# A decoder block on one core: when the third feed-forward layer's weights are loaded, and where the last pair's norm steps stand

## The chip, the core and the metric

The kernel runs on one core of a Trainium2 chip. A core has five engines, each with its own instruction queue that is worked off in order: PE (TensorE, matrix products), DVE (VectorE), ACT (ScalarE), POOL (GpSimd) and SP (SyncE, here only for sending DMAs). They wait for each other through semaphores. Operands lie in the on-chip memory SBUF, PE writes to PSUM, and 16 DMA engines move data from and to HBM. A DMA can be sent from SP, ACT or POOL; one sent from POOL occupies POOL while it is issued.

The metric is the device time in microseconds (us) of one execution, as the median of several runs. The profile comes from one more execution; its times count from the first instruction (the span's start).

## What is computed

A decoder block on `x` of 32 sequences, 128 tokens and 256 features: causal linear self-attention, cross-attention to a context, and a gated feed-forward network, each behind a layer norm and added to `x`. Cut to the part that matters here:

```python
def ffn(x, w1_w, w1_s, w2_w, w2_s, h1_w, h1_s, h2_w, h2_s, w3_w, w3_s):
    tlin = lambda x, w, s: jnp.einsum('bsi,oi->bso', x, w) * s
    h = silu(tlin(x, w1_w, w1_s)) * tlin(x, w2_w, w2_s)      # 256 -> 1024, the gate
    h = gelu(tlin(h, h1_w, h1_s))                            # 1024 -> 1024
    h = gelu(tlin(h, h2_w, h2_s))                            # 1024 -> 1024
    return tlin(h, w3_w, w3_s)                               # 1024 -> 256

x = x + linear_attention(layernorm(x), ...)
x = x + cross_attention(layernorm(x), context, ...)
x = x + ffn(layernorm(x), ...)
```

The feed-forward weights are small whole numbers, the rest is float32.

## The kernel before

**Stages.** The 32 sequences are 16 pairs for the two attentions and 8 blocks of four sequences (512 tokens) for the feed-forward network. A loop over 20 steps (`for m in range(STEPS)`) runs the attentions as a pipeline over the pairs: in step m the self-attention works on pair m, the cross-attention on pair m - 3, and the norm's statistics on the pairs behind and ahead. Then a loop over the 8 blocks (`for blk in range(NBLK)`) runs the feed-forward network.

**Order.** What each step emits, and in which order, is written out by hand in lists of units (`both`, `close`, `begins`, `alone`, `last`, `rest`), one list a step; `give` walks a list. Most functions are generators: every mention of a unit in a list runs it up to its next `yield`, so that PE's part, ACT's part and POOL's part of one unit can stand apart. PE, ACT, DVE and POOL execute in just the order in which the code emits (`manual_schedule`).

**Filling.** While the last attention steps leave PE free, parts of block 0 of the feed-forward network are run early: `fills` holds its input (transposes), the 8 column groups of the gate (`ffn_gate`) and the first three column groups c = 0, 1, 2 of H1 (`ffn_gelu`). `beside` starts the next fill (its matmuls), `settle` finishes those begun (activation and split).

**Split.** Products run in fp32r, with the activations as a sum of two parts, each multiplied by the same weights. `split` makes them: `gh` (or `sh`, `xh`) is the value cast by POOL, `gl` (`sl`, `xl`) the remainder, taken by the engine passed as `low_engine`: in the fills that is POOL, afterwards DVE. `hidden` multiplies: for each of the 8 slices k of a weight, one matmul with the high and one with the low part. So a column group of H1 or H2 takes 16 matmuls, and each of them needs gh and gl of one column group of the layer before. The unsplit `hg` and `hs` share three buffers.

**Norm.** `norms(k)` holds, for the pairs that end a stage in step k, the statistics (`bn_stats` on DVE), the start of the inverse square root on DVE (`deviations` up to its `yield`, lines 147 to 152), and three Newton steps of four small operations each on POOL (lines 156 to 162), which write `devs`. In the last step, k = 19, only pair 15 is left, whose statistics serve the feed-forward norm of block 7. There the unit is mentioned six times: the first two only pass empty parts, the third runs the statistics and the start, the fourth the Newton steps, the other two nothing.

**Weights of the feed-forward network.** W1, W2 and H1 are loaded during the attentions. H2 (8 slices of 512 KB) and W3 (8 slices of 128 KB) lie in memory that the cross-attention held until then: after the step loop, `left.close()` releases it, and new pools are opened there (lines 845 to 849). The tile framework gives each load the waits for what was there before (`reuse_waits="tile"`): in the built program the first H2 load waits for eight semaphores of earlier SP and ACT loads, one of an earlier POOL load, and one of PE, for the last `pf` matmul of the cross-attention. `load_some` (line 859) sends up to three of the 16 slices, from POOL, and `layer` calls it ahead of each column group (line 870): in block 0, H1 continues with c = 3, so the first three slices are sent ahead of the column group c = 3, the next three ahead of c = 4, and so on. POOL's DMAs take eight semaphores in turn, and a DMA waits until the one before it on its semaphore has landed; so the load of W3 slice k waits for H2 slice k.

POOL's order before, from the last cross-attention add (line 662): gh and gl of c = 2, twelve Newton operations, H2 x3, gh of c = 3, H2 x3, gh of c = 4, H2 x2 and W3 x1, gh of c = 5, W3 x3, gh of c = 6, W3 x3, gh of c = 7, W3 x1.

Of the kernel before, what the change touches and what calls it, by code (L numbers as in the profile page):

```python
# [22 lines left out]
HC = HID // P  # L23
# [5 lines left out]
STEPS = NPAIR + SKEW + 1  # L29
# [18 lines left out]
def decoder_block_kernel(  # L48
# [14 lines left out]
    nc = tc.nc  # L63
# [24 lines left out]
    C_PAR, C_PARS, C_BQ, C_BK, C_W1, C_W2, C_H1, C_H2 = 0, 2, 4, 6, 8, 16, 24, 32  # L88
# [5 lines left out]
    def batch(b):  # L94
        return xs[b // 2][:, b % 2, :]

    W1, W2, H1 = (
        const.tile([P, w.shape[0] // P, w.shape[1]], F32R, name=n) for n, w in (("W1", w1T), ("W2", w2T), ("H1", h1T))
    )
# [10 lines left out]
    def load(n, dst):  # L110

        which, k, width = FFN_SLICES[n]
        nc.gpsimd.dma_start(out=dst[:, k, :], in_=(w1T, w2T, h1T, h2T, w3T)[which][ts(k, P), :])
# [62 lines left out]
    G_TAGS = X_TAGS + ["r20", "r21"] + [f"l{i}" for i in range(10)]  # L176
# [5 lines left out]
    def temporary(tag, name, bufs):  # L182
        return hid["r"].tile([P, TB], F32, tag=tag, name=name, bufs=bufs)
# [6 lines left out]
    def split(t, name, tags, high_engine=nc.gpsimd, low_engine=nc.vector):  # L190

        high, low = part(f"{name}h", tags[0]), part(f"{name}l", tags[1])
        (high_engine.copy if high_engine is nc.scalar else high_engine.tensor_copy)(high, t)  # L193
        lows.append(lambda: low_engine.tensor_tensor(low, t, high.bitcast(F32), ALU.subtract))  # L194
        return high, low

    def finish():
        while lows:
            lows.pop(0)()
# [13 lines left out]
    def ffn_input(xns, res):  # L213
        pts = []
        for c in range(DC):
            pt = ffn_bank("pt")
            for j in range(NB):
                nc.tensor.transpose(pt[:, ts(j, S)], xns[j // 2][:, j % 2, ts(c, P)], ident)  # L218
            pts.append(pt)
        yield  # L220
        for c in range(DC):
            res.append(split(pts[c], "x", X_TAGS[2 * c : 2 * c + 2], nc.scalar))
        finish()

    def hidden(w, src, c):
        pp = ffn_bank("ph")
        for k, parts in enumerate(src):
            for p in range(2):
                nc.tensor.matmul(  # L229
                    pp,  # L230
                    lhsT=w[:, k, ts(c, P)],
                    rhs=parts[p],
                    start=(k == 0 and p == 0),
                    stop=(k == len(src) - 1 and p == 1),
                )
        return pp

    def ffn_gate(src, c, res, low_engine=nc.vector):

        one, two = hidden(W1, src, c), hidden(W2, src, c)  # L240
        yield
        sil = temporary("sil", "sil", 2)
        nc.scalar.activation(sil, one, AF.Silu, scale=col[:, C_W1 + c : C_W1 + c + 1])  # L243
        t = temporary("h", "hs", 3)
        nc.vector.scalar_tensor_tensor(t, two, col[:, C_W2 + c : C_W2 + c + 1], sil, ALU.mult, ALU.mult)  # L245
        finish()
        res.append(split(t, "s", S_TAGS[2 * c : 2 * c + 2], low_engine=low_engine))

    def ffn_gelu(w, src, c, c_scale, tags, res, low_engine=nc.vector):
        pp = hidden(w, src, c)  # L250
        yield
        t = temporary("h", "hg", 3)
        nc.scalar.activation(t, pp, AF.Gelu, scale=col[:, c_scale + c : c_scale + c + 1])  # L253
        res.append(split(t, "g", tags[2 * c : 2 * c + 2], low_engine=low_engine))
        finish()

    def whole(parts):
        for _ in parts:
            pass
# [13 lines left out]
    with tc.manual_schedule(engines=ORDERED):  # L273
# [413 lines left out]
        def settle():  # L687
# [105 lines left out]
        rest = [  # L793
            (b_weighted, -1, 1), (b_weighted, -1, 1), (norms, 0), (b_weighted, -1, 1), (norms, 0),
            (b_weighted, -1, 1), settle, beside, (b_out, -1, 1), (b_out, -1, 1), (b_out, -1, 1), settle,
            (norms, 0), (norms, 0), (norms, 0), (norms, 0),
        ]

        def give(units, m):
# [18 lines left out]
        under_way = {}  # L818
        FILLS = 1 + HC + 3
        block, begun = {"x": [], "s": [], "g": []}, []  # L820
        fills = [lambda: ffn_input(block["xn"], block["x"])]
        fills += [lambda c=c: ffn_gate(block["x"], c, block["s"], nc.gpsimd) for c in range(HC)]
        fills += [lambda c=c: ffn_gelu(H1, block["s"], c, C_H1, G_TAGS, block["g"], nc.gpsimd) for c in range(FILLS - 1 - HC)]

        Bs[0]["c"] = cT0
        done = {(b_load, 0)}
# [25 lines left out]
        def weights(n):  # L852
            return (W1, W2, H1, H2, W3)[FFN_SLICES[n][0]]
# [5 lines left out]
        def load_some():  # L859
            for _, n in zip(range(3), loading):  # L860
                load(n, weights(n))

        def raw():
            return temporary("sil", "raw", 2)

        def layer(blk, w, src, c_scale, tags, res):

            waiting = None
            for c in range(len(res), HC):
                load_some()  # L870
                parts = ffn_gelu(w, src, c, c_scale, tags, res)
                if (blk or w is H2) and c % 4 == 0:
                    n = next(testing, None)
                    waiting = None if n is None else (weights(n), *again(raw, n))
                whole(parts)
                if waiting and c % 4 == 3:
                    test(*waiting)
# [18 lines left out]
        for blk in range(NBLK):  # L896
# [13 lines left out]
            block = {"x": [], "s": [], "g": []}  # L910
# [147 lines left out]
```

## Time and profile before

| | us |
|---|---|
| median of 3 runs | 1097.52 |
| lowest and highest | 1096.7 and 1099.23 |
| the profiled execution | 1099.32 |
| its span, first to last instruction | 1097.3 |
| PE, busy in the span | 1081.9 |
| DVE, busy | 609.9 |
| POOL, busy | 416.4 |
| ACT, busy | 377.8 |
| first H2 load issued, at | 472.3 |
| third layer of block 0 begins on PE, at | 481.8 |
| mean TensorE clock granted, of full speed | 0.996 |

How to read it: the step loop takes the first 464 us or so, the feed-forward blocks the rest. The page's second part shows PE at 9 tenths or more in nearly every slice, from the first to the last:

```profile
PE   8999999999999999999999999999999999999997
DVE  5888888888888877523433433433433432423421
POOL 4565555555555446652312312312312312312311
DMA  7001000011110000050010010010011000000000
```

Each digit is the busy share, in tenths, of one fortieth of the span (27 us). The DMA row's 5 is the slice from about 466 to 494 us: the loads of H2 and W3. The kind of each load and its time from issue to landing (KB each, median us):

```profile
H<-in_h1T_dram POOLq DMA_DIRECT2D x8, 512.0 KB, 3.6
H<-in_h2T_dram POOLq DMA_DIRECT2D x8, 512.0 KB, 7.2
W<-in_w3T_dram POOLq DMA_DIRECT2D x8, 128.0 KB, 5.6
```

H1's slices, sent one at a time, take 3.6 us; H2's, sent together, 7.2 in the median.

### The profile page before, as it was taken

To read this page: it belongs to the slowest core of one execution; us is meant where nothing else is said; L and a number is where in the kernel's file an instruction comes from. 1 tells how busy PE (TensorE), PEld (TensorE's weight loads), DVE (VectorE), ACT (ScalarE), POOL (GpSimd) and SP (SyncE) were. 2 spreads that over 40 slices of the span, in tenths; PEclk is the share of its full clock that TensorE was granted. 3 is DMA by queue.
4 is the path that set the end of the run, shared out by engine and by line. 5 is a ranking of instruction groups with operands and counts; after the bars stand their busy time and mean duration, and the time that the engine had idled before them with its cause. 6 is when DMAs were issued, how large, how long until landed. Compare 5 with 4: busy or idle time off the path is not lost.

```text
span 1097.3 us, 19468 instructions
## 1 busy us (share of the span) xinstructions
PE 1081.9 (99%) x7990; PEld 878.0 (80%) x7990; DVE 609.9 (56%) x1249; ACT 377.8 (34%) x594; POOL 416.4 (38%) x778
## 2 busy tenths in 40 slices
PE   8999999999999999999999999999999999999997
PEld 6777777777777777778888888888888888888886
DVE  5888888888888877523433433433433432423421
ACT  3234444444444459722322312322322312222221
POOL 4565555555555446652312312312312312312311
PEclk9999999999999999999999999999999999999999
DMA  7001000011110000050010010010011000000000
GB/s 265 1 30 31 30 31 30 31 30 42 38 31 30 12 11 1 21 192 24 34 39 29 30 39 30 29 39 35 24 39 39 20 30 20 10 10 20 11 1 22
DMA packets 26544, 39.23 MB, mean 36 GB/s; under 512 B 2512, under 2 KB 18640, under 8 KB 26448
## 3 DMA queue, kind: packets, MB, share of 16 engines
q1 hardware_dynamic: 22000, 26.09, 7.1%
q0 software_dynamic: 4032, 11.54, 3.3%
q8 instruction: 65, 1.06, 0.4%
q14 instruction: 31, 0.25, 0.1%
q10 hardware_dynamic: 416, 0.28, 0.1%
HBM read 33.71 MB, written 4.19 MB: 35 GB/s over the span
## 4 chain that ended last, share of the span: by engine, by line
PE 92%; POOL 3%; DVE 2%; DMA 1%; issue 1%; ACT 0%; POOLq 0%; DVEq 0%; ACTq 0%
PE ph L229 51%; PE pp L373 10%; PE py L882 6%; PE pf L418 5%; PE pv L381 5%; PE sa L402 4%; PE sm L402 3%; PE se L402 3%; PE pw L381 2%; PE pt L362 1%; DVE at L541 1%; PE pot L657 1%; DMA H<-in_h2T_dram 1%; PE se L633 1%; PE pz L618 1%; PE pt L218 1%
## 5 line engine op out<-in xcount | busy, mean ns | idle before, releaser
L194 DVE TENSOR_TENSOR gl<-hg,gh 128x512 fp32r<-128x512 f32 x125 | 86.9, 695 | 336.5 <-POOL gh L193 333.6
L193 POOL CAST gh<-hg 128x512 fp32r<-128x512 f32 x128 | 79.5, 621 | 359.6 <-ACT hg L253 359.6
L253 ACT ACTIVATE hg<-ph,col 128x512 f32<-128x512 f32 x128 | 88.3, 690 | 365.0 <-PE ph L229 364.9
L229 PE MATMUL ph<-gh,H 128*128 128x512 f32 x512 | 200.3, 391 | 1.1 <-POOL gh L193 0.6
L229 PE MATMUL ph<-gl,H 128*128 128x512 f32 x512 | 200.3, 391 | 0.2 <-DVE gl L194 0.2
L229 PE MATMUL ph<-sh,H 128*128 128x512 f32 x512 | 199.6, 390 | 0.0
L229 PE MATMUL ph<-sl,H 128*128 128x512 f32 x512 | 199.2, 389 | 0.0
L229 PEld LDWEIGHTS ph<-gh,H 128*128 128x128 f32 x512 | 96.6, 189 | 22.0 <-POOL gh L193 1.1
L229 PEld LDWEIGHTS ph<-gl,H 128*128 128x128 f32 x512 | 96.7, 189 | 20.7 <-DVE gl L194 0.5
L229 PEld LDWEIGHTS ph<-sh,H 128*128 128x128 f32 x512 | 96.1, 188 | 20.4 <-issue 0.5
L229 PEld LDWEIGHTS ph<-sl,H 128*128 128x128 f32 x512 | 96.1, 188 | 19.9
L229 PE MATMUL ph<-xh,W 128*128 128x512 f32 x256 | 100.7, 393 | 0.0
L229 PE MATMUL ph<-xl,W 128*128 128x512 f32 x256 | 99.8, 390 | 0.0
L193 POOL CAST sh<-hs 128x512 fp32r<-128x512 f32 x64 | 58.7, 917 | 67.5 <-DVE hs L245 67.5
L541 DVE TENSOR_TENSOR at<-sa,causal 128x1024 f32<-128x1024 f32 x64 | 74.5, 1206 | 15.2 <-PE sa L402 11.9
L608 DVE TENSOR_REDUCE nm<-sm 128x8 f32<-128x1024 f32 x64 | 75.0, 1213 | 12.2 <-PE sm L402 12.2
L644 ACT ACTIVATE pr<-se 128x1024 f32<-128x1024 f32 x64 | 62.0, 1020 | 30.2 <-PE se L633 30.2
L245 DVE SCALAR_TENSOR_TENSOR hs<-ph,col,sil 128x512 f32<-128x512 f32 x64 | 47.9, 749 | 41.3 <-PE ph L229 20.7
L500 ACT ACTIVATE e<-pp,col 128x256 f32<-128x256 f32 x64 | 26.9, 471 | 127.4 <-PE pp L373 96.8
L243 ACT ACTIVATE sil<-ph,col 128x512 f32<-128x512 f32 x64 | 44.1, 690 | 74.9 <-PE ph L229 74.8
L373 PE MATMUL pp<-xTa,WA 128*128 128x256 f32 x256 | 62.5, 388 | 0.7 <-ACT xTa L365 0.7
L882 PE MATMUL py<-W,gh 128*128 128x256 f32 x256 | 62.6, 285 | 0.0
(131 smaller groups left out, 1839.0 us busy)
## 6 DMA issues: line engine op xcount, KB each, us to landing
x<-in_x_dram SPq DMA_DIRECT2D x16, 256.0 KB, 5.5
cT<-in_ctxT_dram SPq DMA_DIRECT2D x16, 256.0 KB, 2.6
H<-in_h1T_dram POOLq DMA_DIRECT2D x8, 512.0 KB, 3.6
H<-in_h2T_dram POOLq DMA_DIRECT2D x8, 512.0 KB, 7.2
out_dram<-y SPq DMA_DIRECT2D x32, 128.0 KB, 1.7
raw<-in_h1T_dram SPq DMA_DIRECT2D x16, 256.0 KB, 2.6
raw<-in_h2T_dram SPq DMA_DIRECT2D x16, 256.0 KB, 2.6
WA<-in_wattn_dram SPq DMA_DIRECT2D x4, 256.0 KB, 4.8
```

The costliest lines, as they stand in the source:

```text
L193: (high_engine.copy if high_engine is nc.scalar else high_engine.tensor_copy)(high, t)
L194: lows.append(lambda: low_engine.tensor_tensor(low, t, high.bitcast(F32), ALU.subtract))
L229: nc.tensor.matmul(pp, lhsT=w[:, k, ts(c, P)], rhs=parts[p], start=(k == 0 and p == 0), stop=(k == len(src) - 1 and p == 1),)
L253: nc.scalar.activation(t, pp, AF.Gelu, scale=col[:, c_scale + c : c_scale + c + 1])
L373: nc.tensor.matmul(pp[:, c, :], lhsT=w[:, d, ts(c, P)], rhs=src[:, d, :], start=(d == 0), stop=(d == DC - 1))
L381: nc.tensor.matmul(pp, lhsT=src[:, d, :], rhs=w[:, d, :], start=(d == 0), stop=(d == DC - 1))
L402: nc.tensor.matmul(sc[g // 2][:, g % 2, 2 * c : 2 * c + 2, :], lhsT=loaded[32 * g : 32 * g + 32, c, ts(j, S)], rhs=streamed[32 * g : 32 * ...
L418: nc.tensor.matmul(pf[32 * g : 32 * g + 32, i, :], lhsT=v[:, 8 * (i // 2) + 2 * g + i % 2, :], rhs=weights[g // 2][:, g % 2, i, :], start= ...
L541: nc.vector.tensor_tensor(at.rearrange("p g i s -> p (g i) s"), sc[u].rearrange("p g i s -> p (g i) s"), causal.unsqueeze(1).to_broadcast( ...
L608: nc.vector.tensor_reduce(nm[:, 2 * u : 2 * u + 2, :], sc[u], AX.X, ALU.max, negate=True)
L644: nc.scalar.activation(pr, sc[u], AF.Exp)
L882: nc.tensor.matmul(py[:, :D], lhsT=h[k][p][:, ts(j, S)], rhs=W3[:, k, :], start=(k == 0 and p == 0), stop=(k == HC - 1 and p == 1),)
```

## The change

Three edits.

- In the last step's list `rest`, the unit `(norms, 0)` is mentioned three times in place of six: it stops behind the start of the inverse square root.
- Right behind the opening of the new pools, `load_some` is called twice, which sends H2 slices 0 to 5 in a row; then the rest of `norms(19)`, the Newton steps, is emitted. `layer` goes on with what is left: H2 slices 6 and 7 and W3 slice 0 ahead of c = 3, W3 slices 1 to 3 ahead of c = 4, 4 to 6 ahead of c = 5, 7 ahead of c = 6.
- The remainder gl of the third H1 fill (c = 2) is taken by DVE, those of c = 0 and 1 by POOL as before.

POOL's order then: gh of c = 2, H2 x6, twelve Newton operations, H2 x2 and W3 x1, gh of c = 3, W3 x3, gh of c = 4, W3 x3, gh of c = 5, W3 x1, gh of c = 6, gh of c = 7. On DVE, gl of c = 2 stands between the last transpose of the cross-attention (line 450) and the last pair's statistics (line 139). The order on PE, ACT and SP is the same, and so are the waits of the first H2 load.

```diff
         rest = [
             (b_weighted, -1, 1), (b_weighted, -1, 1), (norms, 0), (b_weighted, -1, 1), (norms, 0),
             (b_weighted, -1, 1), settle, beside, (b_out, -1, 1), (b_out, -1, 1), (b_out, -1, 1), settle,
-            (norms, 0), (norms, 0), (norms, 0), (norms, 0),
+            (norms, 0),
         ]
...
-        fills += [lambda c=c: ffn_gelu(H1, block["s"], c, C_H1, G_TAGS, block["g"], nc.gpsimd) for c in range(FILLS - 1 - HC)]
+        fills += [
+            lambda c=c: ffn_gelu(H1, block["s"], c, C_H1, G_TAGS, block["g"], nc.vector if c > 1 else nc.gpsimd)
+            for c in range(FILLS - 1 - HC)
+        ]
...
         def load_some():
             for _, n in zip(range(3), loading):
                 load(n, weights(n))
+
+        for _ in range(2):
+            load_some()
+
+        whole(under_way.pop((norms, STEPS - 1)))
 
         def raw():
             return temporary("sil", "raw", 2)
```

## The prediction

> **What bounds the kernel now.** I read the page's busy row first, then the chain of waits, then the timelines of POOL and PE where that chain leaves PE. Columns of the chain: start, length in us, what; of a timeline: start, length, engine, line, operation, count, and in brackets the idle time before it with its releaser.
>
> ```profile
> PE 1081.9 (99%) x7990; PEld 878.0 (80%) x7990; DVE 609.9 (56%) x1249; ACT 377.8 (34%) x594; POOL 416.4 (38%) x778
> ...
> 467.06 1.29 POOL gl L194
> 474.59 1.53 POOL H L113 x3
> 476.63 8.41 DMA H<-in_h2T_dram
> 487.25 27.52 PE ph L229 x113
> 514.77 3.83 PE py L882 x32
> ```
>
> PE is the bound, and after 487 us the chain is PE alone to the end: what moves there moves the end one for one. The stretch that isn't PE runs from 464.3 to 487.3: POOL's work, the issue of the H2 loads, then their landing. But most of that stretch is slack, since PE has the second layer (H1) to do meanwhile. What is lost must be read from PE:
>
> ```profile
> 484.34 0.39 PE L229 MATMUL ph<-gl,H 128*128 128x512 f32 x1
> 485.18 0.47 PE L229 MATMUL ph<-gh,H 128*128 128x512 f32 x1 [0.45 <-DMA H<-in_h2T_dram]
> 485.48 0.40 PE L229 MATMUL ph<-gl,H 128*128 128x512 f32 x1
> 486.53 0.50 PE L229 MATMUL ph<-gh,H 128*128 128x512 f32 x1 [0.65 <-POOL gh L193]
> 487.25 0.50 PE L229 MATMUL ph<-gl,H 128*128 128x512 f32 x1 [0.22 <-DVE gl L194]
> 487.59 0.48 PE L229 MATMUL ph<-gh,H 128*128 128x512 f32 x1
> 487.86 0.63 PE L229 MATMUL ph<-gl,H 128*128 128x512 f32 x1
> ```
>
> Third layer, first column block: 16 matmuls from 481.83, a (gh, gl) pair for each slice k = 0 to 7 of H2. Starts are 0.227 apart until 484.34. Then PE waits for slice 6 of H2, and for gh and gl of k = 7. The next block should begin at 481.83 + 16 x 0.2267 = 485.46 and begins at 487.59: **2.13 us lost by waiting**. Then starts are 0.43 apart until 490.85, and the clock says why (stretch: busy time and count of PE, PEld, DVE, ACT, POOL; then PEclk, DMA share, GB/s):
>
> ```profile
> 440.08:443.49 3.41, 2.33 (x44) 1.58 (x46) 3.31 (x6) 3.29 (x4) 2.36 (x5) 1.00 0.02 5
> 484.45:487.86 3.41, 2.09 (x7) 0.97 (x6) 1.35 (x4) 0.07 (x1) 1.82 (x4) 0.98 1.17 310
> 487.86:491.27 3.41, 3.41 (x10) 2.67 (x9) 1.32 (x3) 0.61 (x1) 0.62 (x1) 0.52 0.16 39
> ```
>
> The stretch with the pauses is followed by one of equal length at half clock. The tenth matmul after 487.59 starts at 491.46: 3.87 for 10 steps instead of 2.27, so **1.60 us more**. Together 3.73 us.
>
> Why did slice 6 and gh of k = 7 come so late? POOL:
>
> ```profile
> 466.37 0.61 POOL L193 CAST gh<-hg 128x512 fp32r<-128x512 f32 x1 [1.25 <-ACT hg L253]
> 467.06 1.29 POOL L194 TENSOR_TENSOR gl<-hg,gh 128x512 fp32r<-128x512 f32 x1
> ...
> 472.26 1.71 POOL L113 DMA_DIRECT2D H<-in_h2T_dram  x3 [0.62 <-issue]
> 473.95 0.64 POOL L193 CAST gh<-hg 128x512 fp32r<-128x512 f32 x1
> 474.51 1.61 POOL L113 DMA_DIRECT2D H<-in_h2T_dram  x3
> ...
> 484.06 0.53 POOL L113 DMA_DIRECT2D W<-in_w3T_dram  x1 [0.69 <-DMA H<-in_h2T_dram]
> 485.32 0.53 POOL L113 DMA_DIRECT2D W<-in_w3T_dram  x1 [0.73 <-DMA H<-in_h2T_dram]
> 485.85 0.62 POOL L193 CAST gh<-hg 128x512 fp32r<-128x512 f32 x1
> ```
>
> The 12 small Newton operations on `t` and `devs` fill 468.31 to 471.64 (the "..."); only then is the first H2 load issued. The second cost is POOL's order: the issue of W3 slice k waits until H2 slice k has landed (they share a semaphore), and gh of k = 7 stands behind W3 slice 6, thus behind H2 slice 6 (landed 485.04).
>
> **The change part by part.**
>
> *gl of c = 2 goes from POOL to DVE.* POOL is rid of 1.29 us. On DVE the operation takes 0.69 to 1.05 us (its rows at 476.77 and 474.62) and starts when gh is cast, 466.98. It stands ahead of the last pair's statistics, which end by about 467.7 + 1.8 = 469.5 instead of 466.34: DVE had nothing to do until 474.62, so this is hidden. PE reads this gl only at 482.96. Cost nothing; if that cover were gone, 1 us.
>
> *Newton behind six loads.* Its 12 operations (3.33 us) are not removed, they leave the way of loads 0 to 5. Their result is read by the norm of the last block only (the last of those reads starts at 975.7). Nothing to pay there.
>
> *Six loads at once.* The first H2 load now follows the cast that ends at 466.98; with the same 0.62 for its waits (ten semaphores; the newest is that of the last `pf` matmul, done at 459.76) it starts at 467.60 instead of 472.26, **4.66 us earlier**. Six issues take 0.63 + 0.54 + 3 x 0.55 + 0.57 = 3.39: to 470.99. Newton to 474.32. Then loads 6 and 7 and W3 slice 0 (0.56 + 0.57 + 0.58): to 476.03.
>
> *Landings.* Before, slices 0 to 7 landed 3.6, 5.2, 7.8, 9.0, 10.3, 11.5, 12.8 and 14.0 us after the first issue (issue plus time to landing); the last six are 1.2 to 1.3 apart, the queue being full. Loads 6 and 7 are issued at 474.3, some 5 us before slice 5 lands (479.1), so the queue doesn't run dry: slice 6 at 480.4, slice 7 at 481.6. PE wants slice 6 at 484.55 and slice 7 at 485.00. That wait goes.
>
> *What queues behind.* gh of c = 3 now comes at 476.03, two us later than 473.95. PE wants it at 483.2. ACT does earlier: `hg` has three buffers, so ACT's hg of c = 6 (478.40) needs gl of c = 3, done at 476.03 + 0.65 + 0.75 = 477.4: 1 us spare. Next, W3 slices 1 to 3 (by 477.8), gh of c = 4 (by 478.5), W3 slices 4 to 6; slice 6 must wait for H2 slice 6: 480.4 + 0.28 + 0.53 = 481.2. Then gh of c = 5 (481.85), W3 slice 7 behind H2 slice 7: 481.6 + 0.28 + 0.53 = 482.4, then gh of c = 6 (483.05), gh of c = 7 (483.75) and its gl on DVE (484.45). PE wants gh of c = 6 at 484.55, gl at 484.78; gh of c = 7 at 485.00, gl at 485.23. All in time, by 0.7 us at the tightest. Written with L for the landing of H2 slice 7: the last gl reaches PE at L + 2.9, so no wait as long as L is below 482.3.
>
> *Sum.* Loads 4.66 earlier, but only the wait can be gained: -2.13, and -1.60 where the half-clock stretch followed. Against the profiled execution (1099.32 = span 1097.3 + 2.0 around it): 1095.6. The median shown, 1097.52, lies 1.80 below the profiled run, about one stretch of 3.41 us at half clock (1.7); the highest of the three, 1099.23, lies 1.71 above the median. I take it that the median run had the waits, not that half-clock stretch. That fits: the stretch must be less than some share busy, between the 61% (2.09 of 3.41) that was followed by half clock and the 68% (2.33) that was not; the three pauses span 484.73 to 487.25, 2.52 us, and all lie in one stretch of 3.41 for only 0.89/3.41 = 26% of its possible positions, if these vary between executions. So from the median only 2.13 comes off: **1095.4 us**.
>
> The Trainium skill speaks against my reading of the clock ("TensorE: Matmul & The Clock Gate", section "What's actually happening"): half clock comes after at least one idle window of some 3.4 us. The trace agrees on the length and on the half, not on the condition, as no window here was idle. By the rule the half-clock stretch has another cause and stays: the changed kernel's profile would then lose 2.13 alone, 1097.2; from the median the sum is the same.
>
> Against moving gl: "SBUF — State Buffer", section "Who interferes with whom" of the Trainium skill has a DVE operation with two SBUF inputs block a GpSimd one that reads SBUF. If it held the first issue for gl's whole 0.69, L would be 482.3, still in time; here gl at 474.62 ran beside three issues that took 1.61, against 1.71 without it.
>
> **The rivals.**
>
> *A, forecast: the waits go, the median had no half-clock stretch there.* 1095.4, 64%.
>
> *B: as A, but the median run had the stretch.* 1097.52 - 3.73 = 1093.8. For it: the profiled run had it. Against: the 1.80 between the two. 19%.
>
> *C: part of the wait stays.* The landing steps are not even (2.6 us between slices 1 and 2, with the queue full). If L comes between 482.3 and 484.35, PE still waits, with 0 to 2 us left: 1095.5 to 1097.5, say 1096.4. Here belongs too that the loads are issued early and land hardly earlier. 11%.
>
> *D, the other side: the POOL queue holds the casts longer.* Before, gh of c = 6 stood behind H2 slice 3 and gh of c = 7 behind slice 6; now both stand behind slice 7. Should L stay where it was (477.2 + 9.1 = 486.3), the last gl reaches PE at 489.2 instead of 487.25: 1097.52 + 1.95 = 1099.5. It decides from L = 484.35, 2.75 later than I have it. For it only the unexplained step of 2.6; against it the released memory (pf done at 459.76) and DMA engines that stand idle until 473. 6%.
>
> **How the numbers follow.** About 0.2% (2.2 us, below 1095.3) can be told from no change. A lies at that bound; as executions of the kernel before that do catch the stretch pull its time up and the difference with it, I put 36 of A's 64 beyond it. Faster 0.36 + 0.19 = 0.55, same 0.28 + 0.11 = 0.39, slower 0.06. Range: from B less 0.4 (1093.4) to nearly no gain in C (1097.2); D and the ends are left out. A alone: 1094.9 to 1095.9.
>
> **What would show it.** Right: first H2 issue near 467.6, Newton between the sixth and seventh, slice 7 landed before 482.3, matmul starts 0.227 apart from 481.8 through the first block of H2, no idle time there by H, gh or gl, granted clock 1.00 in the 7 us that follow. Wrong: an idle row on gh or gl behind a W3 issue (C or D), a first issue after 470, or a half-clock stretch without a pause before it.

## The result, and the profile after

| | before | changed |
|---|---|---|
| median, us | 1097.5 (14 runs) | 1095.61 (14 runs) |
| lowest and highest, us | 1096.02 and 1099.85 | 1094.41 and 1096.35 |
| ratio, 95% interval | | 0.9981, [0.9972, 0.9989] |
| the profiled execution, us | 1099.32 | 1094.41 |
| its span, us | 1097.3 | 1092.6 |
| mean clock granted in it | 0.996 | 0.999 |

The kernel became 0.19% faster, 1.9 us; the interval lies wholly below 1. The two profiled executions lie 4.9 us apart, since one is among the slowest of its kernel and the other the fastest of its own; the waits have to be compared place by place.

The chain of waits of the changed kernel, over the window from 463 to 492 us (start, length, what), is one piece:

```profile
462.81 29.37 PE ph L229 x129
```

Before, POOL, the DMA and DVE set the pace between 464.3 and 487.3. Now PE goes through on its own. PE's timeline at the end of the first column block of H2:

```profile
483.08 0.39 PE L229 MATMUL ph<-gh,H 128*128 128x512 f32 x1
483.31 0.40 PE L229 MATMUL ph<-gl,H 128*128 128x512 f32 x1
483.55 0.39 PE L229 MATMUL ph<-gh,H 128*128 128x512 f32 x1
483.77 0.45 PE L229 MATMUL ph<-gl,H 128*128 128x512 f32 x1
484.06 0.40 PE L229 MATMUL ph<-gh,H 128*128 128x512 f32 x1
```

No row has idle time in brackets. The starts are 0.23 apart but for one step of 0.29: the matmul of 483.77 is drawn out by 0.06, as the last gl comes just then (DVE is done with it at 483.67). The block begins at 480.36, so its 16 steps lose 484.06 - 480.36 - 16 x 0.2267 = 0.07 us, against 2.13 before. Call this loss S. The clock (stretch, busy times, then PEclk, DMA share, GB/s) stays whole in the block after it:

```profile
483.99:487.62 3.63, 3.63 (x17) 2.98 (x17) 1.67 (x5) 0.69 (x1) 0.62 (x1) 1.00 0.00 0
```

POOL's timeline, with the loads ahead of Newton and the casts that stand behind the W3 loads:

```profile
464.87 0.61 POOL L193 CAST gh<-hg 128x512 fp32r<-128x512 f32 x1 [1.25 <-ACT hg L253]
465.71 3.29 POOL L113 DMA_DIRECT2D H<-in_h2T_dram  x6 [0.22 <-issue]
468.96 0.25 POOL L156 TENSOR_TENSOR t<-devs 128x2 f32<-128x2 f32 x1
...
478.34 0.53 POOL L113 DMA_DIRECT2D W<-in_w3T_dram  x1 [1.12 <-DMA H<-in_h2T_dram]
479.57 0.53 POOL L113 DMA_DIRECT2D W<-in_w3T_dram  x1 [0.70 <-DMA H<-in_h2T_dram]
480.10 0.63 POOL L193 CAST gh<-hg 128x512 fp32r<-128x512 f32 x1
480.82 0.53 POOL L113 DMA_DIRECT2D W<-in_w3T_dram  x1
481.34 1.18 POOL L193 CAST gh<-hg 128x512 fp32r<-128x512 f32 x2
```

The first H2 load is issued 14.66 us before PE begins the third layer; in the kernel before it was 9.57 (481.83 - 472.26). W3 slices 5, 6 and, by a last 0.1 us, 7 (480.82) still wait for H2 slices with the casts queued behind them, but now early enough.

### The profile page after: what moved, and what is told of

Same layout as the page of the kernel before. It is cut to its first block, busy times and chain, and to the rows that moved or that the text cites. A ratio compares the mean times of both kernels' runs of the same rounds, so it can differ in the third digit from the quotient of the medians.

```text
span 1092.6 us, 19468 instructions
## 1 busy us (share of the span) xinstructions
PE 1077.9 (99%) x7990; PEld 875.3 (80%) x7990; DVE 610.7 (56%) x1250; ACT 377.6 (35%) x594; POOL 414.5 (38%) x777
## 3 DMA queue, kind: packets, MB, share of 16 engines
q8 instruction: 65, 1.06, 0.4%
## 4 chain that ended last, share of the span: by engine, by line
PE 94%; DVE 2%; POOL 2%; issue 0%; DMA 0%; ACT 0%; SPq 0%; POOLq 0%; DVEq 0%
PE ph L229 53%; PE pp L373 10%; PE py L890 6%; PE pf L418 5%; PE pv L381 5%; PE sa L402 4%; PE sm L402 3%; PE se L402 3%; PE pw L381 2%; PE pt L362 1%; DVE at L541 1%; PE pot L657 1%; PE se L633 1%; PE pt L218 1%; PE pz L618 1%
## 5 line engine op out<-in xcount | busy, mean ns | idle before, releaser
L890 PE MATMUL py<-W,gl 128*128 128x256 f32 x256 | 62.0, 283 | 0.0
```

The lines of the kernel that those rows point to most:

```text
L890: nc.tensor.matmul(py[:, :D], lhsT=h[k][p][:, ts(j, S)], rhs=W3[:, k, :], start=(k == 0 and p == 0), stop=(k == HC - 1 and p == 1),)
```

## The experiments

All against the kernel before, on the same chip as it. S is worked out as above; "first load" and "slice 7" are the issue of the first H2 load and the landing of the last one (its issue plus its time to landing), in us from the start of the third layer on PE, all from the profiled execution. Times to landing are given to a tenth of a us, so "slice 7" is good to about 0.05, and the last digit of the other columns can differ by one from what the printed rows give. 2.13 us is 0.0019 of the time, and the intervals of the ratio are 0.0009 to either side (0.0014 for the second Newton).

| kernel | first load | slice 7 | S | median | ratio |
|---|---|---|---|---|---|
| before | -9.57 | +4.43 | 2.13 | 1097.5 | |
| before again | -9.59 | +4.39 | 2.12 | 1097.22 | 1.0003 |
| gl on DVE alone | -8.55 | +5.33 | 3.01 | 1098.74 | 1.0017 |
| Newton twice | -6.19 | +7.39 | 5.04 | 1102.03 | 1.0044 |
| late W3, else as before | -9.57 | +4.73 | 1.73 | 1096.58 | 0.9994 |
| loads alone (gl on POOL) | -13.53 | +1.38 | 1.32 | 1096.0 | 0.9988 |
| changed | -14.66 | +0.16 | 0.07 | 1095.61 | 0.9981 |
| changed, again | -14.66 | +0.25 | 0.13 | 1095.52 | 0.9985 |
| three loads early | -14.62 | +0.75 | 0.00 | 1095.82 | 0.9986 |
| changed, late W3 | -14.62 | -0.51 | 0.00 | 1095.64 | 0.9982 |
| loads alone, late W3 | -13.53 | +0.98 | 0.00 | 1095.14 | 0.9978 |

**gl on DVE, nothing else.**

```diff
-            ... G_TAGS, block["g"], nc.gpsimd)
+            ... G_TAGS, block["g"], nc.vector if c > 1 else nc.gpsimd)
```

> The kernel before with gl of c = 2 on DVE and nothing else changed. S is the delay of the second H2 column block on PE against an even pace (2.13 us in the kernel before). Theory (what counts is when the first H2 load is issued): the Newton steps wait for the statistics, and these now stand behind gl on DVE; in the changed kernel they ended 2.45 us after the cast of gh, which here is 469.4, so Newton begins at 469.4 instead of 468.3, the first load comes 1.1 us LATER, S = 3.2, time about 1098.6 (ratio 1.001). Rival (each edit brings its own share, POOL being rid of 1.29 us): first load 1.3 us earlier, S = 0.8, time 1096.2 (ratio 0.9988).

Measured 1098.74, ratio 1.0017 [1.0008, 1.0027], S = 3.01. POOL's timeline says why:

```profile
465.82 0.61 POOL L193 CAST gh<-hg 128x512 fp32r<-128x512 f32 x1 [1.25 <-ACT hg L253]
468.80 0.19 POOL L156 TENSOR_TENSOR t<-devs 128x2 f32<-128x2 f32 x1 [2.37 <-DVE hv L152]
...
472.73 1.69 POOL L113 DMA_DIRECT2D H<-in_h2T_dram  x3 [0.62 <-issue]
```

POOL is rid of 1.29 us of work and idles 2.37 us instead, until the statistics that now stand behind gl on DVE are done; the first load goes out 1.0 us later. This edit by itself makes the kernel slower. It gains only where Newton has left the way.

**Newton twice.**

```diff
-        for _ in range(NEWTON):
+        for _ in range(steps):
...
-        yield from deviations(mv[:, cols], means[:, k, cols], devs[:, k, cols])
+        yield from deviations(..., steps=NEWTON * (1 + (k == STEPS - 1)))
```

> The kernel before with the last pair's Newton steps done six times instead of three (12 more operations on POOL, 3.3 us, ahead of the first H2 load; the result converges to the same value). Theory (the first issue sets the stall, one for one, from 2.75 us before the kernel before on): first load 3.3 us later, S = 2.13 + 3.3 = 5.4, time 1100.8, and 1.6 more if a half-clock stretch now always follows: 1100.8 to 1102.4, ratio 1.003 to 1.0045. Rival (POOL has slack there, the loads' own length counts): 1097.5 to 1098.5.

Measured 1102.03, ratio 1.0044 [1.003, 1.0057]; S = 5.04, 2.9 more for 3.4 us of later issue. What POOL does ahead of the first load is paid on PE nearly one for one. The median rose by more than that, 4.7 us: the profiled execution, 1099.85 at a mean clock of 0.999, is the only one of the five without the half-clock extra; the other four took 1102.0 to 1103.0 at 0.994 to 0.995.

**Loads alone: six loads, Newton behind them, gl left on POOL.**

```diff
-            (norms, 0), (norms, 0), (norms, 0), (norms, 0),
+            (norms, 0),
...
+        for _ in range(2):
+            load_some()
+
+        whole(under_way.pop((norms, STEPS - 1)))
```

> The changed kernel with gl of c = 2 left on POOL: six loads at once, Newton behind them. Theory: the first load waits 1.29 us more than in the changed kernel, whose last gl reached PE with nothing to spare; so slice 7 lands 1.3 us later and PE waits 1.3 us for the last gl: S = 1.3, time 1096.8 (ratio 0.9993). Rival (gl of c = 2 doesn't matter, the Newton steps were the whole obstacle): no wait on PE, 1095.5, ratio 0.9981.

Its S was as expected, 1.32; its median of 1096.0 was 0.8 lower than expected. The main wait on PE is not for the last gl, though, but for that of c = 6, which comes 1.06 us after its turn (484.87):

```profile
485.93 0.50 PE L229 MATMUL ph<-gl,H 128*128 128x512 f32 x1 [0.60 <-DVE gl L194]
```

Two more executions of this kernel were profiled, to tell whether the first had been an unusual one:

> The loads-only kernel (six loads, Newton behind them, gl of c = 2 on POOL) once more, one look: its profiled execution lost 1.32 us on PE, yet its median is only 0.2 to 0.4 above that of the kernels that lose nothing. Theory (the lost time varies with how late slice 7 of H2 lands, 13.6 to 15.4 us after the first issue in the profiles so far): this look shows another S, between 0.3 and 1.3, in step with the landing. Rival (it always loses 1.3, and the median is low by scatter elsewhere): S = 1.3 again.

> As the look before, a third execution of the same kernel: theory S between 0.3 and 1.3 with the landing of slice 7 (L after the first load's issue, S = L - 13.6 or so), rival S = 1.3.

S was 0.95 and 1.03, with slice 7 landed 14.6 us after the first issue in both (14.9 in the first profile): in step with L - 13.6, but with little spread. So this kernel lost 1.0 to 1.3 us here in all three profiles. The same kernel with late W3 (below) loses nothing, and its ratio is 0.0010, or 1.1 us, lower: that fits, but the two intervals overlap, so the times alone do not show it. The low median against the expectation is within what the intervals leave open.

**Three loads early instead of six.**

```diff
-        for _ in range(2):
-            load_some()
+        load_some()
```

> The changed kernel with three H2 loads ahead of the Newton steps instead of six. Theory (the queue of three 512 KB loads takes longer to empty than the 3.3 us of Newton, so landings are set by the first issue): slice 7 lands within 0.5 us of where it does in the changed kernel (14.8 us after the first issue), S under 0.5, time 1095.5, ratio 0.9981 to 0.9986. Rival (six in a row are needed): loads 3 to 7 are issued 1.7 to 3.3 us later and land as much later, S = 1.7 to 3.3, time 1097.1 to 1098.8.

No loss on PE (S = 0.00), 1095.82, ratio 0.9986 [0.9977, 0.9995]. Six in a row were not needed. The outcome was the theory's, its reason wasn't: counted from the first issue, loads 3 to 5 go out 3.8 us later than in the changed kernel, and the queue did run short (slice 3 lands 3.7 us after its own issue, as a load sent alone does, and 2.4 after slice 2 instead of some 1.2). Slice 7 came at +0.75 instead of +0.16. It cost nothing because the edit also moves the remaining loads by one column group, and with them the casts. POOL's timeline:

```profile
481.74 0.53 POOL L113 DMA_DIRECT2D W<-in_w3T_dram  x1 [0.70 <-DMA H<-in_h2T_dram]
482.26 0.63 POOL L193 CAST gh<-hg 128x512 fp32r<-128x512 f32 x1
482.98 0.53 POOL L113 DMA_DIRECT2D W<-in_w3T_dram  x1
483.50 0.63 POOL L193 CAST gh<-hg 128x512 fp32r<-128x512 f32 x1
```

The cast of c = 6 (482.26) now stands ahead of the last W3 load and only that of c = 7 behind it, so the last gl came 2.2 us after slice 7 landed, not 3.2 as in the changed kernel. What three early loads cost with the casts in the changed kernel's order, this run doesn't show.

**Late W3: the W3 loads sent from the third layer's column groups**, so that no cast of the second layer queues behind a landing.

```diff
-        loading, testing = iter(late), iter(range(len(FFN_SLICES)))
+        loading, testing = list(late), iter(range(len(FFN_SLICES)))
...
-        def load_some():
-            for _, n in zip(range(3), loading):
-                load(n, weights(n))
+        def load_some(upto=len(FFN_SLICES)):
+            for _ in range(3):
+                if loading and loading[0] < upto:
+                    n = loading.pop(0)
+                    load(n, weights(n))
...
-                load_some()
+                load_some(len(FFN_SLICES) if w is H2 else len(FFN_SLICES) - HC)
```

In the kernel before:

> The kernel before with the W3 loads sent from the third layer's column groups, so that no cast of the second layer stands behind a landing. Theory (two waits: slices 6 and 7 of H2 land late, and the last cast is held by POOL's order): the cast of c = 7 comes early, PE waits for slices 6 and 7 alone (landing 485.0 and 486.3), S = 1.4 instead of 2.1, time 1096.8, ratio 0.9993. Rival 1 (POOL's order is nearly all of it): S = 0.5, 1095.9. Rival 2 (landing is all of it): S = 2.1, no change, 1097.5.

1096.58, ratio 0.9994 [0.9985, 1.0003], S = 1.73. PE's timeline, idle time and releaser in brackets:

```profile
485.18 0.47 PE L229 MATMUL ph<-gh,H 128*128 128x512 f32 x1 [0.55 <-DMA H<-in_h2T_dram]
485.49 0.40 PE L229 MATMUL ph<-gl,H 128*128 128x512 f32 x1
486.41 0.47 PE L229 MATMUL ph<-gh,H 128*128 128x512 f32 x1 [0.52 <-DMA H<-in_h2T_dram]
486.72 0.40 PE L229 MATMUL ph<-gl,H 128*128 128x512 f32 x1
```

The waits for gh and gl are gone; a wait for slice 7 itself has taken their place. So landings and POOL's order were two stalls, one behind the other, and taking away the order alone gets 0.4 us, or up to 0.7 if one allows for slice 7, which happened to land 0.3 later here (+4.73 against +4.43). On the time alone this run would have told nothing.

In the changed kernel, and in the loads-alone kernel:

> The changed kernel with the W3 loads sent from the third layer's column groups. The casts no longer stand behind landings; the last gl, which reached PE with nothing to spare, comes when ACT's hg of c = 7 allows it, some 1 us earlier. Theory (the changed kernel has no wait left here): same time as the changed kernel, ratio 0.9981 against the kernel before; on PE no lost step at all. Rival (tight timing still costs in some executions): 0.3 to 0.5 us less than the changed kernel.

> The loads-only kernel with the W3 loads sent from the third layer's column groups: slice 7 of H2 lands as late as in the loads-only kernel, but no cast stands behind it. Theory (there the landing itself was in time, only the casts behind it were late): S = 0 to 0.1, time that of the changed kernel, ratio 0.9981 to 0.9986. Rival (the landing itself is late): S as in the loads-only kernel.

Both S = 0.00, with 0.9982 [0.9973, 0.9991] and 0.9978 [0.9969, 0.9988]. The second lands slice 7 at +0.98, nearly as late as the loads-alone kernel (+1.08 to +1.38), and loses nothing: there it was the casts that were late, not the weights. The changed kernel once more, beside it:

> The changed kernel once more beside the loads-only one with late W3. Theory: S = 0 to 0.2, ratio 0.998; the last gl arrives within 0.5 us of when PE wants it. Rival: in other executions it waits by more than 0.5 us.

S = 0.13, ratio 0.9985 [0.9975, 0.9994]. Neither late-W3 version is faster than the changed kernel by more than the intervals.

**The kernel before once more, for the clock.**

> The kernel before, unchanged, for the granted clock of each execution. Theory (half-clock stretches fall where the position of the stretches allows it, each costs about 1.6 us): the times fall into steps of some 1.2 to 1.7 us, in step with the mean clock (0.996 for two stretches, 0.9975 for one), and fewer than half of the executions have the one at the H2 wait. Rival (the clock has nothing to do with the scatter): no relation of time and clock.

Nine of 11 executions took 1097.0 to 1097.8, two 1099.2 and 1099.5. Its profiled execution (1097.0) has the same waits (S = 2.12) and no half clock behind them:

```profile
483.80:487.20 3.40, 2.09 (x8) 0.99 (x7) 1.34 (x4) 0.06 (x1) 1.84 (x4) 1.00 1.08 284
487.20:490.60 3.40, 3.40 (x16) 2.80 (x15) 1.34 (x3) 0.63 (x1) 0.61 (x1) 1.00 0.17 42
```

Over all 98 timed executions of the kernel before, 84 lie below 1098.0, 14 above 1099.0 and none between. The mean clock of an execution did not sort the lower group (1097.0 at 0.999, 1097.1 at 0.996), so that part of the expectation fell; the twelve of the upper group whose clock is on record all show 0.996. The two profiles of this kernel, 2.3 us apart with the same waits, say where such a difference arises: 0.6 before the third layer (481.83 against 481.19; the slower one has half clock from 20.1 to 23.5 too), and the 1.6 behind the pauses.

## Why the prediction was right

*The place and the size of the gain.* The prediction took 2.13 us of waits off the median, to 1095.4; it came to 1095.61. The medians differ by 1.9, and S went from 2.13 to 0.07 or 0.13. The interval is 0.09% to either side, finer than the 0.2% that the chances went by, so these 1.9 us can be told from no change. The chain from the first issue to the last gl holds in both directions: 1.0 us later gives S = 3.0, 3.4 later 5.0, 5.1 earlier nothing.

*Leaving the half-clock stretch out.* This choice (case A against B) decided the number, and it held: only 14 of 98 executions of the kernel before lie some 2 us above the rest, and the profile of 1097.0 has the waits without the half clock. The profiled run of before, 1099.32, belongs with the 14. The 26% worked out from positions was too many (14%), but on the right side; the positions themselves no run shows.

*gl of c = 2 at no cost.* True in the changed kernel, where Newton stands behind the loads. What it costs when that cover is gone was put at "1 us"; alone it costs 0.9 us of S, through the statistics and not, as the sentence there read, through gl itself.

*First issue at 467.60.* It came 0.23 us after the cast, not 0.62, so 14.66 us ahead of the third layer instead of 14.23.

*Landings and slack: the step that was mis-sized.* "All in time, by 0.7 us at the tightest": there was nothing left, S = 0.07 and 0.13. Two terms are responsible. Slice 7 landed 14.8 and 14.9 us after the first issue, not 14.0. And L + 2.9 was too short: the last gl came at L + 3.2, since gl of c = 6 took 1.07 us instead of 0.69 (below). The first issue, 0.4 earlier, took part of it back: 0.8 + 0.3 - 0.4 = 0.7, just the slack that the prediction had. That nothing was lost is therefore luck in part. The loads-alone kernel, 1.1 us later, shows the edge passed: S = 1.0 to 1.3. One sum on the way is off as well: from 476.03, a cast and three W3 issues end at about 478.2, not "by 477.8", and gh of c = 4 at 478.8, not 478.5; the wait for slice 6 at 480.4 hides it.

*Rivals.* C did not happen in the changed kernel; the loads-alone kernel is what C describes. D's mechanism, the casts queued behind W3 and so behind slice 7, is real and is all that the loads-alone kernel pays, but slice 7 landed at +0.16, 2.4 us before the point from which the prediction let D decide (484.35, which is +2.52).

## What to carry to other kernels

A busy engine's idle row names the releaser that came last; behind it may stand a second one, nearly as late. Remove one wait in a trial and look at what takes its place, as with the W3 loads here.

Work that nobody needs soon, on a queue that sends loads, costs what it delays. And an edit that frees one queue can lengthen it through the work it displaces on the other: two edits that gain together need not gain alone.

Before taking a profile's loss off a median, see whether the profiled execution is a typical one.

## What the runs showed of the hardware

**Half clock after a partly idle stretch.** How often an execution takes some 2 us more than the others of its kernel grows with what PE loses: none of 56 (the five runs with S below 0.2), none of 24 (S = 1.0 to 1.7), 14 of 98 (S = 2.1), 4 of 11 (S = 3.0, clock 0.995 to 0.996, the others 0.997 to 0.999), 4 of 5 (S = 5.0, clock 0.994 to 0.995). Only one profile, that of the kernel before, shows the half-clock stretch behind the pauses itself; in the other executions it is inferred from the time and the mean clock. The longest single pause of PE in these blocks is 0.65 us in any profile, so the Trainium skill's condition ("TensorE: Matmul & The Clock Gate", section "What's actually happening": at least one idle window) is too strict for the stretch seen here. That the position of the stretches decides was only argued.

**A remainder on DVE waits for a cast on POOL.** DVE's timeline of the changed kernel:

```profile
480.76 0.69 DVE L194 TENSOR_TENSOR gl<-hg,gh 128x512 fp32r<-128x512 f32 x1 [3.27 <-POOL gh L193]
482.00 1.07 DVE L194 TENSOR_TENSOR gl<-hg,gh 128x512 fp32r<-128x512 f32 x1 [0.55 <-POOL gh L193]
```

The second began 0.1 us after POOL's next cast (481.90 to 482.52) and ended 0.55 after it; the same operation took 1.07 in the loads-alone kernel too (484.80), again beside a cast. This agrees with the rule of the Trainium skill ("SBUF — State Buffer", section "Who interferes with whom") that a DVE operation with two SBUF inputs and a GpSimd one that reads SBUF exclude each other. The prediction weighed this rule for the load issue, where gl took 0.69 beside it (465.52), and not for the casts, where it took part of the slack. Not every remainder beside issues took 0.69: that of c = 3 took 1.12 in the changed kernel (474.65) and 1.05 in the one before, beside three issues and no cast; why stays open.

**A fetch of code among the loads.** In eleven of the 13 profiles one transfer of 16 KB on the instruction queue falls into the loads, 4.5 to 6.0 us before the third layer begins on PE, wherever the loads are. DMA queues of the changed kernel, window 475 to 477 us (packets, MB, share of 16 engines):

```profile
q0 software_dynamic: 208, 0.75, 108.3%
q8 instruction: 1, 0.02, 2.9%
```

It takes some 0.93 us on one DMA engine (2.9% of 16 engines over 2 us), and the H2 slice under way lands 2.2 to 3.3 us after the one before instead of 1.2. In the kernel before it fell together with another such step (+4.7 us after the first issue, steps of 1.6 and 2.6), in the changed one apart from it (+9.8, steps of 2.2 and 2.5): 14.8 instead of 14.0. With Newton twice, where it fell before the first load's data, slice 7 took 13.6. With gl on DVE alone, where it fell into the first load, it was 13.9. That this transfer delays the loads is thus a reading of where it falls; no run isolates it.
